# Layer 0: dt's products on four column groups of the array, and residual adds moved to TensorE and ScalarE

## The chip, the cores and the metric

The kernel runs on one core of one Trainium2 chip. The metric is the device time of one execution in microseconds (us), as the median of several runs. Engines are named as the profile names them: PE is TensorE's matmul, PEld its weight load, DVE is VectorE, ACT is ScalarE, POOL is GpSimd, SP is the queue that only issues DMAs. All data are float32.

## The reference, cut to what matters

The network has four layers of the form x = x + layer(groupnorm(x)) on an input of 1024 channels by 64 x 64. The change touches layer 0 alone, where the 1024 channels are also the sequence of a decaying sum:

```
def layer0(x, log_A, dt_w, dt_b, ln_w, ln_b):     # x after the group norm: [1, 1024, 64, 64]
    x_norm = layernorm2d(x, ln_w, ln_b)           # per channel, over the 64 x 64 image
    A = -exp(log_A)                               # one per image row
    dt = softplus(einsum('bsdc,c->bsd', x_norm, dt_w[0]) + dt_b[0])   # a sum over the 64 columns
    cums = cumsum(dt * A, axis=1)                 # along the channels
    M = exp(cums_t - cums_j) for t >= j, else 0   # per image row
    return einsum('btjr,bjrc->btrc', M, x_norm)
x = x + layer0(groupnorm(x))
```

dt is one number per channel and image row. The sum with M is a scan along the channels: out[t] = exp(dt[t] A) out[t-1] + x_norm[t]. Layers 1 to 3, mainly large matmuls, need mean and variance of layer 0's result first.

## The kernel before, in words

**Units and pieces.** Layer 0 works on 8 units u: four chunks of 256 channels (2 tiles k of 128 channels), each in two halves of the image (32 rows). A unit has 16 blocks of 128 pixels (32 rows by 4 columns), in 4 pieces g of 4 blocks. So there are 32 pieces, i = 4u + g, and the main loop (L753) runs once a piece.

**The steps of a piece.** A tile holds channels on its partitions. normalize (L581) writes xn, the group norm and layer norm in one scale and bias, on GpSimd for all but the first twelve. turn_in (L598) turns eight 128x128 blocks on TensorE into PSUM (tile xpt, two buffers), and ScalarE (in the first pieces partly VectorE) copies them to xt with ln_w and ln_b (four instructions of 128x256). Now pixels are on the partitions and channels along the row. row_dt (L617) makes dt: four products a piece, sixteen accumulated in PSUM tile pd of a unit; the weights dtm (128x128) hold dt_w and sum over the four columns of an image row and at once spread the sum to the four partitions of that row. decay (L625) is in three steps: step 0, four ScalarE instructions, makes softplus in two parts, e and m; step 1 adds them on TensorE, by two products with the identity, into the other half of pd; step 2 makes exp(A dt) (ScalarE, tiles first and a). begin (L646, GpSimd) puts the end of the chunk before into the first column. scan (L653, VectorE) runs two scans of 128x512. turn_back (L672) turns the eight blocks back into PSUM (tile pb, two buffers, one for each k), and add_up (L686) adds them to the image in place, with the sum of the result (VectorE; two instructions of 128x512). squares (L699, ScalarE) takes a finished tile's squares for the variance.

**by_act.** For k = 1 of pieces 25 to 30 the residual add goes otherwise (by_act, L665): TensorE first puts the image's piece into PSUM by a product with the identity (L676), then adds the four blocks by plain products instead of transposes (L682), and ScalarE copies the sum back with its total (L695).

**What sets the order.** The engines' orders are written out by hand (manual_schedule, L515): each engine runs its instructions in the order of the program. turn_in runs LEAD = 7 pieces ahead of scan, row_dt 6. In the loop's body the order is: normalize (for odd i, two tiles), decay step 1 (at g = 2), scan of i, add_up of i - 1, turn_in of i + 7, row_dt of i + 6, turn_back of i, decay step 0 of unit u + 1 (g = 1), decay step 2 and begin of unit u + 1 (g = 2), statistics of later units (VectorE, up to i = 11), one step of the next chunk's group norm (from i = 3 and 11), squares of unit u - 1 (g = 0 and 1), and one step of sums. sums (L711) prepares weights of layers 1 and 2 in the meantime: every four pieces four additions on GpSimd (L456 to L459), with their loads and stores on SP's queue. GpSimd's queue thus has, unit by unit: begin, the four additions, normalize.

Of the kernel before, what the change touches and what calls it, by code (L numbers as in the profile page):

```python
# [10 lines left out]
F32 = mybir.dt.float32  # L11
# [9 lines left out]
P = 128  # L21
# [16 lines left out]
NK = -(-N // LT)  # L38
# [27 lines left out]
T0 = HN // P  # L66
TR = HW // 2
TW = HW // T0
CH = 2
NPIECE = T0 // 4  # L70
# [4 lines left out]
        ("Alog", S), ("D", 1), ("mob", 4 * HEADS), ("dbcb", HEADS * NF)]  # L75

_CST = [("ident", P), ("fold", LC), ("same", P), ("upto", LC), ("far", LC), ("eye", LC), ("eye8", S),
        ("from", 1), ("to", NK), ("group", P), ("row", P),
        ("gx", NT), ("gy", NT), ("flip", 7)]


# [9 lines left out]
CST, NCST = _columns(_CST)  # L91
# [3 lines left out]
def tile_net(ctx: ExitStack, tc: tile.TileContext, x, par_d, cst_d, w_d, w2_d, dbcw_d, out):  # L95
    nc = tc.nc
# [23 lines left out]
    cst = const.tile([P, NCST], F32, name="cst")  # L120
    par = const.tile([P, NPAR], F32, name="par")
    ident = cst[:, CST["ident"]]
# [388 lines left out]
    with tc.issue_after(exp_ln.ins), tc.tile_pool(name="l0x", bufs=2) as lx, \  # L511
# [4 lines left out]
        NU, NI = CT // CH * 2, CT // CH * 2 * NPIECE  # L516
# [27 lines left out]
        negA0 = const.tile([P, 2], F32, name="negA0")  # L544
        nc.scalar.activation(negA0, par[:, PAR["logA"]], AF.Exp)
        negA = const.tile([P, S], F32, name="negA")
        nc.scalar.activation(negA, par[:, PAR["Alog"]], AF.Exp)
        dtm = l0.tile([P, T0, P], F32, name="dtm", bufs=1)
        for t in range(T0):
            nc.gpsimd.tensor_scalar(dtm[:, t, :], cst[:, CST["row"]], pcol("dtw", t), None, ALU.mult)  # L550
        carry = l0.tile([P, 2, T0], F32, name="carry", bufs=1)
# [24 lines left out]
            nc.vector.tensor_copy(mean0[:, at], mean)  # L576
            nc.vector.tensor_scalar_mul(nmean0[:, at], mean, -1.0)

        xn, XT, PD, dt, PB = {}, {}, {}, {}, {}

        def normalize(n):  # L581

# [34 lines left out]
        def row_dt(i):  # L617
            u, g = divmod(i, NPIECE)
            if g == 0:
                PD[u] = ps0.tile([P, FB], F32, tag="pd", name=f"pd{u}")  # L620
            for j in range(4):
                t = 4 * g + j
                nc.tensor.matmul(PD[u][:, : CH * P], dtm[:, t, :], XT[i][:, j, :], start=(t == 0), stop=(t == T0 - 1))  # L623

        def decay(u, step):  # L625

            if step == 0:
                e = l0.tile([P, CH * P], F32, tag="e", name=f"e{u}", bufs=1)
                m = l0.tile([P, CH * P], F32, tag="m", name=f"m{u}", bufs=1)
                dt[u] = e, m  # L630
                v = PD[u][:, : CH * P]
                nc.scalar.activation(e, v, AF.Abs, bias=pcol("dtb", 0))
                nc.scalar.activation(e, e, AF.Exp, scale=-1.0)
                nc.scalar.activation(m, v, AF.Relu, bias=pcol("dtb", 0))
                nc.scalar.activation(e, e, AF.Ln, bias=1.0)
            elif step == 1:
                for i, v in enumerate(dt[u]):
                    nc.tensor.matmul(PD[u][:, CH * P :], ident, v, start=(i == 0), stop=(i == 1))
            else:
                v, scale = PD[u][:, CH * P :], negA0[:, u % 2 : u % 2 + 1]  # L640
                if u > 1:
                    nc.scalar.activation(first_[u % 2], v[:, :1], AF.Exp, scale=scale)
                nc.scalar.activation(spread[u % 2][:, :, 1:], v[:, 1:].unsqueeze(1).to_broadcast([P, 2, CH * P - 1]),
                                     AF.Exp, scale=scale)
# [18 lines left out]
                nc.gpsimd.tensor_copy(carry[:, u % 2, 4 * g : 4 * g + 4], XT[i][:, :, CH * P - 1])  # L663

        def by_act(i, k):  # L665
            return NI - LEAD <= i < NI - 1 and k == 1

        def pieces_of(i, k):
            u, g = divmod(i, NPIECE)
# [42 lines left out]
        LEAD = 7  # L712
# [18 lines left out]
        row_dt(2)  # L731
        unit_stats(3, range(4))
        row_dt(3)
        decay(0, 0)
        normalize(4)
        unit_stats(3, range(4, 8))
# [16 lines left out]
        for i in range(NI):  # L753
            u, g = divmod(i, NPIECE)
            if i > 1 and i % 2 and i + LEAD + 2 < 4 * NU:
                normalize(i + LEAD + 2)
                normalize(i + LEAD + 3)
            if u + 1 < NU and g == 2:
                decay(u + 1, 1)
            scan(i)  # L760
            hand_on(i)
            if i == 0:
                finish_of(chain)
                chain = iter(())
            if i > 0:
                add_up(i - 1)
            if i == 0:
                for v, n in later.pop(0):
                    unit_stats(v, (n,))
                turn_in(5, (2, 3))  # L770
                turn_back(0)
                turn_in(6, (2, 3))
                row_dt(5)
            elif i + LEAD < NI:
                if i == 1:
                    row_dt(LEAD - 1)
                    turn_in(LEAD, (2, 3))
                    normalize(LEAD + 3)
                    normalize(LEAD + 4)
                turn_in(i + LEAD, ())  # L780
            if 0 < i <= NI - LEAD:
                row_dt(i + LEAD - 1)
            if i > 0:
                turn_back(i)
            if i == 0:
                normalize(LEAD + 1)
                normalize(LEAD + 2)
            if u + 1 < NU and g == 1:
                decay(u + 1, 0)
            if u + 1 < NU and g == 2:  # L790
                decay(u + 1, 2)
                if u > 0:
                    begin(u + 1)
            for v, n in later.get(i, ()):
                unit_stats(v, (n,))
            if i in (3, 11):
                chain = norm_chunk(2 if i == 3 else 3)
            next(chain, None)
            if i >= NPIECE and g < CH:
                squares(u - 1, g)  # L800
            if u == NU - 1 and 0 < g:
                for k in range(CH):
                    squares(u, k, g - 1)
            if g == 0 and u % 2 == 1:
                last_keep = keep(u // 2)
            if i == NPIECE + 1:
                bring(6)
            next(sums, None)
# [232 lines left out]
    with tc.manual_schedule(engines={E_.DVE, E_.PE, E_.Pool, E_.Activation}):  # L1041
        for i, _ in enumerate(pointwise("l1", W1, "b1", [3, 2] + EARLY, x0_d, x1_d, scores)):
# [11 lines left out]
            elif i == last - 1:  # L1054
                columns(FIRST, finish_of(chain), norm2)
                mv2 = moments("gn2b", SECOND, range(2))
                name = f"{WX}_{EARLY[0]}"
# [20 lines left out]
    part, silus = {}, []  # L1078
# [21 lines left out]
    with tc.tile_pool(name="l2a", bufs=2) as pa, tc.tile_pool(name="l2a2", bufs=1) as pa2, \  # L1100
# [5 lines left out]
        row = pa2.tile([P, TPB, HEADS, NF2], F32, name="row", bufs=1)  # L1106
# [729 lines left out]
def _constants():  # L1836
    c = np.zeros((P, NCST), np.float32)
    p, j = np.arange(P)[:, None], np.arange(P)[None, :]
    c[:, CST["ident"]] = p == j
    h, r = np.divmod(p, LC)  # L1840
    t = np.arange(LC)[None, :]
    c[:, CST["fold"]] = r == t
    c[:, CST["same"]] = h == j // LC
    c[:, CST["upto"]] = (t < S) | (r <= t)
    c[:, CST["far"]] = np.where((r >= S) & (t >= S) & (t < r), FAR, 0)
    c[:, CST["eye"]] = (r == t) & (r >= S)
    c[:KW, CST["eye8"]] = np.tile(np.eye(S), (KW // S, 1))
    c[:, CST["from"]] = HEADS * N + np.where(r < S, h * S + r, HEADS * S)
    c[:, CST["to"]] = HEADS * N + np.arange(NK)[None, :] * P + p
    c[:, CST["group"]] = (p // 32 == j // 32) / 32  # L1850
    c[:, CST["row"]] = p // TW == j // TW
    s = 1 - 2 * ((np.arange(P)[:, None] >> np.arange(6)[None, :]) & 1)
    s[:, 5] = 1
    c[:, CST["flip"]] = np.concatenate([s[:, :1], -s[:, :1], s[:, :5] * s[:, 1:]], axis=1)
    lin = _side()
    c[:, CST["gx"]] = np.tile(lin, HW).reshape(NT, P).T
    c[:, CST["gy"]] = np.repeat(lin, HW).reshape(NT, P).T
    return c
# [63 lines left out]
```

## Time and profile before

| | us |
|---|---|
| median of 3 runs | 2637.35 (2635.98 to 2638.56) |
| the profiled execution, its own time | 2640.7 |
| its span | 2638.5 |
| layer 0 ends, first matmul of layer 1 (L892) starts | 196.98 |
| first scan (L658) starts | 41.65 |
| one transpose block of turn_in, issue to issue | 0.12 |
| one scan (L658, 64 in all), mean | 1.205 |
| one residual add on VectorE (L697, 58 in all), mean | 0.68 |
| one residual add on ScalarE (L695, 6 in all), mean | 0.58 |
| products of dt (L623, 256 records), busy in all | 64.1 |

A row of the timeline or of the chain gives the start in us from the span's start, the length in us, the engine, the line and the tiles, with "x4" for four instructions in one row. In a row of the windows come, after the stretch and its length, each engine's busy time with its instructions in brackets, then the granted clock of TensorE (1.00 is full), the DMA engines' share and GB/s. A float32 product is two records of TensorE (two passes over the moving data each), a transpose is one. The durations of matmuls are modelled and overlap; the distance from start to start says what one costs.

### The profile page before, as it was taken

How to read it: one execution, taken by the hardware profiler on the slowest of the kernel's cores; microseconds unless marked ns; L12 is line 12 of the kernel's file. 1: busy time of each engine (PE TensorE's matmuls, PEld its weight loads, DVE VectorE, ACT ScalarE, POOL GpSimd, SP SyncE). 2: the span in 40 equal slices, each digit the busy share in tenths (PEclk: the TensorE clock that was granted, in tenths of full speed). 3: DMA queues.
4: the chain of work that ended last, by engine and by line, in shares of the span. 5: the costliest groups of instructions: out<-in, count | busy, mean ns of one | idle time of the engine just before them, and what ended most of it. 6: DMA issues, size and time to landing. Idle time of an engine off the chain costs nothing.

```text
span 2638.5 us, 30736 instructions
## 1 busy us (share of the span) xinstructions
PE 2560.3 (97%) x9588; PEld 1714.0 (65%) x9588; DVE 1819.1 (69%) x3776; ACT 1057.0 (40%) x1799; POOL 1217.9 (46%) x1102
## 2 busy tenths in 40 slices
PE   5889999999999999999999999999999999999999
PEld 5764444444555445544454558888888888788887
DVE  7986775664565554377877766576685775877877
ACT  4672010005655554476867662233233223312120
POOL 2453224322324242256464635576565665754544
PEclk9999999999999999999999999999999999999999
DMA  6555648655655676577677847899898798888896
GB/s 258 184 210 166 230 146 279 205 157 200 188 148 143 155 190 162 179 248 224 206 241 240 283 140 211 220 277 291 236 296 253 247 306 222 290 284 299 301 322 216
DMA packets 426996, 597.22 MB, mean 226 GB/s; under 512 B 142004, under 2 KB 210739, under 8 KB 423764
## 3 DMA queue, kind: packets, MB, share of 16 engines
q1 hardware_dynamic: 307268, 384.68, 46.0%
q10 hardware_dynamic: 91744, 136.85, 14.7%
q0 software_dynamic: 27824, 73.74, 11.7%
q8 instruction: 78, 1.28, 0.2%
q14 instruction: 82, 0.67, 0.1%
HBM read 435.10 MB, written 160.05 MB: 226 GB/s over the span
## 4 chain that ended last, share of the span: by engine, by line
PE 83%; DVE 8%; ACT 5%; POOL 1%; DMA 1%; issue 1%; SPq 0%; ACTq 0%; DVEq 0%; POOLq 0%
PE mm L892 38%; PE q_P2P L1793 6%; PE q_P3P L1793 5%; PE q_P1P L1793 5%; PE q_P5P L1793 5%; PE q_P6P L1793 5%; PE q_P4P L1793 5%; PE q_P7P L1793 5%; PE l2pt L1145 2%; PE py L1430 2%; DVE xt L658 1%; DVE cvp L1126 1%; ACT b L996 1%; DVE stats L567 1%; PE pd L623 1%
## 5 line engine op out<-in xcount | busy, mean ns | idle before, releaser
L892 PE MATMUL mm<-t,w 128*128 128x512 f32 x1536 | 681.0, 594 | 0.0
L892 PE MATMUL mm<-b,w 128*128 128x512 f32 x1152 | 513.6, 597 | 5.1 <-ACT b L996 4.0
L892 PEld LDWEIGHTS mm<-t,w 128*128 128x128 f32 x1536 | 285.8, 190 | 321.4 <-issue 313.6
L892 PEld LDWEIGHTS mm<-b,w 128*128 128x128 f32 x1152 | 215.6, 191 | 252.7 <-issue 240.7
L1439 POOL DMA_INDIRECT y_rows<-g,dst x74 | 74.1, 1001 | 181.8 <-ACT g L1435 169.9
L1126 DVE SCALAR_TENSOR_TENSOR cvp<-xs,par,cvp 128x512 f32<-128x512 f32 x128 | 95.4, 754 | 75.7 <-ACT cvp L1123 73.4
L1762 ACT COPY qQ<-q_P5P 128x512 f32<-128x512 f32 x48 | 28.1, 584 | 296.4 <-PE q_P5P L1793 269.0
L470 POOL TENSOR_TENSOR s<-s 128x256 f32<-128x256 f32 (+3 forms) x120 | 130.2, 1090 | 7.5
L1433 ACT COPY g<-py 8x512 f32<-8x512 f32 x146 | 83.8, 574 | 107.6 <-PE py L1430 106.6
L1177 DVE TENSOR_TENSOR xs<-mm,xs 128x512 f32<-128x512 f32 x64 | 41.8, 685 | 117.9 <-PE mm L892 117.9
L1153 POOL TENSOR_TENSOR acc<-l2xt,acc 128x136 f32<-128x136 f32 x56 | 29.3, 522 | 193.6 <-ACT l2xt L1147 192.7
L1013 DVE SCALAR_TENSOR_TENSOR image<-mm,par,image 128x512 f32<-128x512 f32 x64 | 47.0, 745 | 88.2 <-PE mm L892 88.2
L1145 PEld LDWEIGHTS l2pt<-both,cv 128*128 128x128 f32 x512 | 76.1, 190 | 34.6 <-issue 21.5
L850 POOL TENSOR_TENSOR t<-t,b 128x512 f32<-128x512 f32 x40 | 55.7, 1419 | 88.8 <-DVE t L850 85.4
L996 ACT ACTIVATE b<-image,gnl_bias,gnl_r_r 128x512 f32<-128x512 f32 x48 | 37.0, 808 | 145.4 <-PE mm L892 114.2
L1793 PE MATMUL q_P1P<-t_b,wq_P1P 128*128 128x256 f32 x384 | 92.0, 383 | 2.5 <-POOL t_b L1547 2.5
L1547 POOL TENSOR_TENSOR t_t<-qt 128x512 f32<-128x512 f32 x23 | 29.6, 1288 | 138.9 <-DVE qt L1547 72.4
L1793 PE MATMUL q_P5P<-t_t,wq_P5P 128*128 128x256 f32 x384 | 92.2, 383 | 0.4 <-POOL t_t L1547 0.4
L1793 PE MATMUL q_P4P<-t_t,wq_P4P 128*128 128x256 f32 x384 | 90.9, 380 | 1.4 <-DVE qV L1770 1.4
L1551 ACT ACTIVATE qb<-x_x_b,gn_bias,gn_r_r 128x512 f32<-128x512 f32 x64 | 48.8, 808 | 107.3 <-DVE qQ L1722 36.0
L1770 DVE TENSOR_TENSOR qV<-q_P4P,qV 128x512 f32<-128x512 f32 x96 | 64.8, 686 | 37.7 <-PE q_P4P L1793 36.0
L1793 PE MATMUL q_P6P<-t_t,wq_P6P 128*128 128x256 f32 x384 | 90.7, 379 | 0.0
(432 smaller groups left out, 5962.6 us busy)
## 6 DMA issues: line engine op xcount, KB each, us to landing
w<-s_d SPq DMA_DIRECT2D x96, 512.0 KB, 4.3
w<-in_w_dram SPq DMA_DIRECT2D x72, 512.0 KB, 4.7
x_x_b<-x_d ACTq DMA_DIRECT2D x28, 1024.0 KB, 6.4
image<-x_d SPq DMA_DIRECT2D x12, 2048.0 KB, 12.4
wq_P6P<-s_d SPq DMA_DIRECT2D x84, 256.0 KB, 4.3
wq_P7P<-s_d SPq DMA_DIRECT2D x84, 256.0 KB, 5.5
wq_P5P<-s_d SPq DMA_DIRECT2D x84, 256.0 KB, 3.1
wq_P3P<-s_d SPq DMA_DIRECT2D x84, 256.0 KB, 3.6
```

Source lines behind the costliest of these rows:

```text
L470: eng.tensor_tensor(out, a, b, ALU.subtract)
L850: eng.tensor_tensor(B[name][k], B[one][k], B[two][k], ALU.subtract)
L892: nc.tensor.matmul(to[o], w[:, k, o * P : (o + 1) * P], B[name][k], start=(fresh and k == 0), stop=(k == KH - 1), skip_group_check=True)
L996: nc.scalar.activation(t, X[nb][:, ct, :], AF.Identity, bias=bias, scale=scale)
L1126: nc.vector.scalar_tensor_tensor(cv, xo[:, at + t : at + t + FB], pcol("dww", 3 * o + t), cv, ALU.mult, ALU.add)
L1145: nc.tensor.matmul(pt[:, q * NV : (q + 1) * NV], cv[:, (q0 + q) * P : (q0 + q + 1) * P], both[:, o, :], start=True, stop=True)
L1430: nc.tensor.matmul(py, G2[k % 2], rows[k][:, :DH], start=True, stop=True)
L1433: nc.scalar.copy(rows[k + 1][h * LC : h * LC + S, :DH], py[h * LC : h * LC + S])
L1439: nc.gpsimd.indirect_dma_start(out=y_views[k % len(y_views)][:, :], out_offset=bass.IndirectOffsetOnAxis(ap=dst_[:, k : k + 1], axis=0), i ...
L1551: nc.scalar.activation(tile_of(j, name)[:, k], held[j, "x", name][:, k], AF.Identity, bias=bias, scale=scale)
L1770: nc.vector.tensor_tensor(to, ps, to, ALU.add)
L1793: nc.tensor.matmul(ps[:, o, :], w[:, k, o * P : (o + 1) * P], rhs[:, k, :], start=(new and o == 0 and k == 0), stop=(k == 1), skip_group_c ...
```

## The change

**dt's products.** dtm becomes 32 columns wide: its product gives one row of the result for each image row, without the spreading. The four products of a piece (j = 0 to 3) write four different groups of 32 partitions of pd, so each uses its own group of 32 columns of the array; every group accumulates over the four pieces of the unit. Two new steps make the whole of it: own_rows copies pd (128x256) to SBUF on ScalarE, and all_rows adds the four groups and spreads the rows with one product with a new constant, rows, into the other half of pd. decay reads that half, and its step 1 writes the first half.

**The order.** own_rows of unit u + 1 stands after row_dt and ahead of turn_back of the pieces with g = 1; all_rows after turn_back; then squares of unit u - 1, which at g = 1 were at the end of the body, and then decay step 0.

**The residual adds.** by_act now also holds for k = 1 of pieces 0 to 13. TensorE gets fourteen products with the identity and 56 plain products in place of transposes, ScalarE fourteen adds, VectorE loses fourteen.

```diff
-        ("from", 1), ("to", NK), ("group", P), ("row", P),
+        ("from", 1), ("to", NK), ("group", P), ("row", TR), ("rows", P),
...
-        dtm = l0.tile([P, T0, P], F32, name="dtm", bufs=1)
+        dtm = l0.tile([P, T0, TR], F32, name="dtm", bufs=1)
...
-                nc.tensor.matmul(PD[u][:, : CH * P], dtm[:, t, :], XT[i][:, j, :], start=(t == 0), stop=(t == T0 - 1))
+                nc.tensor.matmul(PD[u][j * TR : (j + 1) * TR, : CH * P], dtm[:, t, :], XT[i][:, j, :],
+                                 start=(g == 0), stop=(g == NPIECE - 1))
+
+        def own_rows(u):
+            part[u] = l0.tile([P, CH * P], F32, tag="m", name=f"part{u}", bufs=1)
+            nc.scalar.copy(part[u], PD[u][:, : CH * P])
+
+        def all_rows(u):
+            nc.tensor.matmul(PD[u][:, CH * P :], cst[:, CST["rows"]], part[u], start=True, stop=True)
...
-                v = PD[u][:, : CH * P]
+                v = PD[u][:, CH * P :]
...
-                    nc.tensor.matmul(PD[u][:, CH * P :], ident, v, start=(i == 0), stop=(i == 1))
+                    nc.tensor.matmul(PD[u][:, : CH * P], ident, v, start=(i == 0), stop=(i == 1))
...
-                v, scale = PD[u][:, CH * P :], negA0[:, u % 2 : u % 2 + 1]
+                v, scale = PD[u][:, : CH * P], negA0[:, u % 2 : u % 2 + 1]
...
         def by_act(i, k):
-            return NI - LEAD <= i < NI - 1 and k == 1
+            return k == 1 and (i < NI - 2 * LEAD - 4 or NI - LEAD <= i < NI - 1)
...
         row_dt(3)
+        own_rows(0)
+        all_rows(0)
         decay(0, 0)
...
                 row_dt(i + LEAD - 1)
+            if u + 1 < NU and g == 1:
+                own_rows(u + 1)
             if i > 0:
                 turn_back(i)
...
             if u + 1 < NU and g == 1:
+                all_rows(u + 1)
+                if i >= NPIECE:
+                    squares(u - 1, g)
                 decay(u + 1, 0)
...
-            if i >= NPIECE and g < CH:
+            if i >= NPIECE and g < CH and not (g == 1 and u + 1 < NU):
                 squares(u - 1, g)
...
-    c[:, CST["row"]] = p // TW == j // TW
+    c[:, CST["row"]] = p // TW == j[:, :TR]
+    c[:, CST["rows"]] = p % TR == j // TW
```

## The prediction

> **What bounds the kernel now.** I read the page's slices first, then a table by stretches, then the chain of waits inside layer 0 (0 to 197 us), where all of the change lies. From 197 us on TensorE hardly pauses:
>
> ```profile
> PE   5889999999999999999999999999999999999999
> DVE  7986775664565554377877766576685775877877
> ```
>
> A slice is 66 us: only the first three of PE are not full. What comes after layer 0 moves with its end, so one us won or lost there is one us of the run. Inside layer 0:
>
> ```profile
> core 0: us, PE busy (x) PEld busy (x) DVE busy (x) ACT busy (x) POOL busy (x), PEclk, DMA share, GB/s
> 41.60:75.20 33.60, 28.46 (x165) 24.87 (x165) 31.86 (x63) 23.27 (x41) 10.68 (x13) 0.95 0.13 49
> 75.20:93.60 18.40, 15.63 (x99) 13.81 (x98) 18.26 (x38) 13.16 (x29) 7.53 (x12) 1.00 0.84 302
> 93.60:113.90 20.30, 16.24 (x97) 14.04 (x96) 20.23 (x39) 13.80 (x27) 14.10 (x23) 0.92 0.35 121
> 113.90:131.80 17.90, 16.91 (x101) 15.04 (x100) 15.38 (x34) 12.29 (x25) 5.87 (x11) 0.90 0.49 174
> 131.80:149.40 17.60, 15.85 (x101) 14.07 (x101) 14.17 (x25) 13.76 (x27) 11.50 (x18) 1.00 0.38 127
> ```
>
> Until 113.9 us VectorE is full (31.86 of 33.60, 18.26 of 18.40, 20.23 of 20.30). Afterwards no engine is full, and yet a unit (four pieces) takes 17.3 us. The chain of waits of one such unit says why:
>
> ```profile
> 126.77 0.16 ACT first L642
> ...
> 127.09 0.32 POOL carry L648
> ...
> 128.15 1.22 POOL s_s L456
> ...
> 133.43 2.37 POOL xn L590 x2
> 135.80 0.04 issue
> 135.85 1.11 PE xpt L607 x7
> 136.96 1.74 PE pd L623 x8
> 138.70 0.02 issue
> 138.72 0.48 ACT e L632
> ...
> 140.31 1.71 ACT junk_None L709
> ...
> 142.30 1.82 ACT xt L615 x4
> 144.12 0.16 ACT first L642
> ```
>
> It is a **ring**: first lets GpSimd begin; that queue then runs the weight sums and the next xn; TensorE needs xn to turn in, then does pd; ScalarE does the decay, the squares, the four xt, and the next first. First starts at 85.68, 103.02, 126.66, 144.00, 161.33 and 175.33 us, so three of five turns are 17.34, 17.34 and 17.33: the ring binds from 85 to 103 us too, level with VectorE. The turn of 23.64 us is set by VectorE and the group norm's small products.
>
> **The change, part by part.**
>
> *VectorE.* One add (its read of the accumulator included) takes 0.60 us: two, as four rows, take 1.20 in the chain. Fourteen fewer: -8.4 us of VectorE, nearly all in stretches where it is full. It counts only where nothing else closes the gap.
>
> *TensorE, dt's products.* Now four products are eight records in 1.74 us a piece, 0.214 each. No product of the trace lies on 32 columns, so I bound it: 0.43 if all four groups run at once (two records after each other), 1.74 if none do. Both records of one product use the same columns, so if records also start in their order, the second of one overlaps only the first of the next: five steps of 0.214, **1.07 us**, the value I take, as it lies between the ends; both ends go into the range.
> The Trainium skill (TensorE: Matmul & The Clock Gate, Part 3) gives 2.38 times for three column tiles, and I estimate from it 0.55 us here; TensorEngine Tiling (Key Properties) speaks against: a switch of the tiling mode drains the array, twice a piece here, without a price.
>
> *TensorE, turning back.* The last pieces already add by TensorE:
>
> ```profile
> 171.08 1.02 PE L676 MATMUL pb<-low,cst 128*128 128x512 f32 x2
> 171.94 0.60 PE L684 MATMUL pb<-cst,xt 128*128 128x128 f32 x4
> 172.38 1.06 PE L682 MATMUL pb<-cst,xt 128*128 128x128 f32 x8
> 173.27 0.38 PE L638 MATMUL pd<-e,cst 128*128 128x256 f32 x1
> ```
>
> By the starts: 0.86 for the identity product, 0.44 for four transposes, 0.89 for four plain products. A piece costs 2.19 instead of 0.87, +1.32. With xpt 0.96, a changed piece takes 0.96 + 1.07 + 2.19 = 4.22 us of TensorE, where it was 3.57. The one residual add left on VectorE waits for the identity product first.
>
> *ScalarE.* Fourteen adds at 0.58 + 0.10 (174.76 to 175.43): they stand before the xt of the next piece and mostly fill waits for TensorE. The eight own_rows are copies of 128x256; the nearest rows are the Relu and Abs of the same shape from PSUM, 0.46 and 0.47. I take 0.47, with 0.58 (the 128x512 copy) as the other end.
>
> *The ring.* Four things happen to its turn.
> (a) pd gets 0.67 shorter, but own_rows stands behind the four xt in ScalarE's queue, and these end 2.53 us after xpt's start (135.85, 138.38), pd at 2.85. So own_rows starts at most 0.3 earlier: -0.3, whatever pd costs below 1.6.
> (b) own_rows: +0.47.
> (c) all_rows (one product, 0.43) comes after turn_back on TensorE and is hidden behind the squares (1.99 + 0.10), which now stand ahead of decay. Uncovered it would cost 0.43 and up to 2.19 of turn_back more.
> (d) The squares used to cover TensorE's answer to decay. TensorE does the sums of e and m (140.37 to 141.33, 0.96) and then xpt; xt starts 0.74 after xpt (144.89 to 145.63). Both now follow decay with nothing on ScalarE but an add: 0.06 + 0.96 + 0.74 = +1.76.
> Sum: -0.3 + 0.47 + 1.76 = **+1.9 us**, a turn of 19.3 instead of 17.34. New waits: ScalarE's for xt, with spread and first behind it, GpSimd behind those; TensorE's for e, 3 us instead of 0.8, with xpt behind it.
> In the changed pieces TensorE alone needs 4 x 4.22 + 0.43 + 0.96 + 2.1 (its wait for e: all_rows ends 4.65 after xpt's start, decay at 6.8) = 20.4 a unit, more than the ring.
>
> *The head.* Up to the first scan, shorter pd lets the statistics start about 1 us sooner; up to 85.68 VectorE loses five adds, -3.0. Against it stand 1.32 of turning back a piece, own_rows, all_rows and the uncovered waits of two decays. With pd at 1.07 the rows run so: turn_back of piece 3 ends at 69.6 (now 68.5); xpt of piece 11 runs to 72.0, in two halves with ScalarE's xt between, since a product of the group norm holds one of its two PSUM tiles (its gap now: 1.17); pd and turn_back take 1.07 + 2.19, to 75.2; xpt of piece 12, in halves again, to 77.7; pd 78.8; own_rows 79.3; squares 81.4; decay 83.0; sums of e and m 84.0; xt 84.7 to 86.5; first at **86.6**. With pd at 0.43 all of it is some 2.5 us earlier, 84. The 32-wide dtm saves GpSimd time before 21 us, where TensorE waits for ScalarE's xn, not for it: nothing. The 96 other columns of the constants: nothing, they land long before use.
>
> *The sum*, as times of first: 86.6 (+0.9); + 20.4 = 107.0 (+4.0); + 20.4 + 0.5 for the group norm's two products = 127.9 (+1.2: this turn was 23.64); + 19.3 = 147.2 (+3.2); + 19.3 = 166.5 (+5.2). Begin follows, and with it scan 24, 0.4 of whose delay an earlier wait had hidden (+4.8). From there VectorE paces the last eight pieces as now; its one wait of 0.72 at 176 goes. End of layer 0: **+4.1 us**, and as much on the run. With pd at 0.43 it starts 2.5 earlier, TensorE needs no more than the ring, and it ends at about 0.
> The profiled execution took 2640.7 (span 2638.5), 3.35 over the median of the runs, 2637.35. Nothing in the sum depends on that, so I add to the median: **2641.4 us**.
>
> **The rivals.** A measurement can tell 0.2%, 5.3 us, from no change.
>
> *The clock halves in the new waits (slower).* Two stretches show where this decides:
>
> ```profile
> 107.18:110.60 3.42, 1.46 (x11) 1.06 (x10) 3.42 (x7) 0.13 (x1) 3.34 (x3) 1.00 0.60 222
> 110.60:114.01 3.41, 2.47 (x8) 2.19 (x9) 3.34 (x9) 2.19 (x5) 3.25 (x6) 0.50 0.39 153
> 69.64:73.05 3.41, 2.08 (x13) 1.87 (x14) 3.41 (x8) 1.40 (x3) 0.55 (x2) 1.00 0.00 0
> ```
>
> 1.46 us busy of 3.42 (43%) was followed by half clock; 2.08 of 3.41 (61%), and 1.73 (51%) at 58 us, were not. With turning back at 0.87, all_rows ends at 3.55 after xpt's start and TensorE then waits till 6.8: 3.2 us idle. Half clock then doubles the e and m sums (+0.87) and half of xpt (+0.44): +1.3 a turn. It decides from a busy share somewhere between 43% and 51%. Two to five turns: 2644 to 2648, on to 2650 with more. Against it: where the windows fall is luck, and a window half in the wait keeps the clock.
> The skill's page on the clock gate (Part 1) has a free-running window of 3413 ns, which agrees with the 3.41 us of half clock here.
>
> *The groups don't overlap (slower; the change doesn't do what it says).* pd stays 1.74: a changed unit on TensorE is 4 x 4.89 + 0.43 + 0.96 + 1.65 = 22.6, +2.2 for two units, +1.5 in the head, +0.3 in the ring: 4.1 + 6.2 = +10.3, 2647.7. For it: no row shows overlap. Against it: the groups write different partitions.
>
> *The relief goes through (faster).* If the ring's waits are shorter than the order of the queues makes them, VectorE is what counts up to 114 us: -8.4, and some of its later 9.3 us of waits for pb goes as well. About -8, 2629. For it: VectorE is full there. Against it: GpSimd waits 25.0 us for first after 113 us alone, and the chain passes through it.
>
> **How the numbers follow.** The forecast (2641.4; 2637 with pd at 0.43) 0.42; half clock 0.25; no overlap 0.16; relief 0.17. The first is within 0.2%; I count both slower rivals as slower and the last as faster: 0.17, 0.42, 0.41. The range 2632 to 2651 leaves out the far half of the faster case and the mixtures of both slower ones, under 2 in 10.
>
> **What would show it.** pd on 32 columns: the spacing of a piece's eight records (0.43, 1.07 or 1.74). The turns of first: 19.3 instead of 17.34 after 126 us. ScalarE idle by about 1.7 us between decay's last step and the next xt. VectorE's adds 44 instead of 58, and waits for pb in pieces 6 to 12. Granted clock 0.5 between 125 and 170 us for the first rival. I am wrong if the turns stay near 17.3, or if first comes well before 84 us in its first turn.

## The result, and the profile after

The changed kernel takes **2643.83 us** (median of nine runs, 2642.00 to 2651.33) against 2637.35 before (median of nine, 2635.09 to 2638.90): a ratio of **1.0025, with a 95% interval of 1.0016 to 1.0034**, or 6.5 us longer. The forecast was 2641.4, 4.1 us longer; the range holds the time, and the loss lies a little beyond the 0.2% that the forecast's own case allowed.

The profiled execution took 2642.14 (span 2640.3), only 1.4 over the one before. That pair misleads. Layer 1's first product starts at 201.87 instead of 196.98, **+4.9 us**. The same instructions of the later layers are 4.2 us late up to 920 us (L351 on VectorE starts at 905.56 instead of 901.33) and 5.0 by 1570 us. The profile before then happens to have two more stretches of half clock in layer 3 (at 1574.9 and 2312.2 us, 3.4 us each), and after each of them the distance has shrunk by some 1.7 us. So layer 0 is where the change must be read, by the start of layer 1's first product; the rest of the span, from there on, takes 2438.0 to 2445.5 us in the fourteen profiles of this study, whatever was done to layer 0.

That start is itself good to a microsecond or two only. Ahead of it stands a row of small steps that make layer 1's group norm; from the first of them (tile mean, behind the last residual add) to the first product it is 6.0 to 8.6 us in the fourteen profiles. One of the steps in the profile before, beside an addition of the weight sums on GpSimd, and the same step in the changed kernel:

```profile
194.40 1.26 POOL L457 TENSOR_TENSOR s_a<-s_a,s_a 128x512 f32<-128x512 f32 x1
194.41 1.26 DVE L174 SCALAR_TENSOR_TENSOR gnl_r_t<-gnl_r_t,gnl_v 128x8 f32<-128x8 f32 x1
...
200.02 0.17 DVE L174 SCALAR_TENSOR_TENSOR gnl_r_t<-gnl_r_t,gnl_v 128x8 f32<-128x8 f32 x1
```

The step took 1.26 us there and 0.17 here. The residual adds themselves end later by more than 4.9: mean starts at 195.46 instead of 189.85, +5.6. Of this 1.1 came back by that step, and 0.4 was added by the first product's wait for its weights (a DMA, by the profile).

The page's slices of the changed kernel are like those shown of before, with small differences: VectorE's second and third are lower (8 7 where it was 9 8) and its fourth higher, as layer 0 ends later, and TensorE's third is lower (7, was 8):

```profile
PE   5879999999999999999999999999999999999999
...
DVE  7877775674565554377877766576585775877876
```

Three of the stretches that were shown of before, in the changed kernel (busy time of PE, PEld, DVE, ACT, POOL, then the clock):

```profile
75.20:93.60 18.40, 14.71 (x111) 10.41 (x109) 15.68 (x31) 13.50 (x33) 6.42 (x12) 1.00 0.65 233
93.60:113.90 20.30, 17.84 (x120) 12.84 (x116) 14.86 (x24) 15.46 (x33) 11.53 (x18) 0.92 0.33 107
...
131.80:149.40 17.60, 12.39 (x91) 8.72 (x91) 12.66 (x23) 13.12 (x26) 9.77 (x17) 0.90 0.35 120
```

VectorE is no longer full: 15.68 of 18.40 and 14.86 of 20.30, where it had 18.26 and 20.23. TensorE is less busy later on (12.39 of 17.60, where it had 15.85). And yet no unit is done sooner; from 131.8 to 149.4 us every engine is idle for a quarter of the time or more (ScalarE, the fullest, is busy for 13.12 of 17.60). The first of each unit starts at 86.79, 106.86, 128.25, 147.39, 167.30 and 180.55 us: turns of 20.07, 21.39, **19.14, 19.91** and 13.25. One such turn in the chain of waits of the changed kernel:

```profile
128.37 0.16 ACT first L650
...
135.03 2.36 POOL xn L590 x2
...
138.16 1.75 ACT xt L615 x4
...
139.97 0.38 ACT part L628
140.35 1.99 ACT junk_None L717 x2
...
143.52 0.31 ACT e L643
...
143.88 1.13 PE pd L646 x4
...
145.58 1.93 ACT xt L615 x4
```

Up to xt at 138.16 it is the ring of before: first, GpSimd up to xn, TensorE, ScalarE. New are own_rows (part, 0.38) and the steps on PE between e and xt (pd, the sums, and then 0.48 of xpt): the chain used to pass from decay through the squares to xt on ScalarE alone. It now goes over to TensorE and back, 143.83 to 145.58, while ScalarE stands still.

### The profile page after: what moved, and what is told of

The parts are those of the page before. It is cut to its first block, busy times and chain, and to the rows that moved or that the text cites. A ratio compares the mean times of both kernels' runs of the same rounds, so it can differ in the third digit from the quotient of the medians.

```text
span 2640.3 us, 30951 instructions
## 1 busy us (share of the span) xinstructions
PE 2551.5 (97%) x9688; PEld 1686.4 (64%) x9688; DVE 1804.8 (68%) x3748; ACT 1068.0 (40%) x1835; POOL 1214.2 (46%) x1102
## 4 chain that ended last, share of the span: by engine, by line
PE 84%; DVE 6%; ACT 6%; POOL 2%; DMA 2%; issue 1%; SPq 0%; ACTq 0%; DVEq 0%; POOLq 0%
PE mm L907 38%; PE q_P2P L1808 6%; PE q_P3P L1808 5%; PE q_P5P L1808 5%; PE q_P1P L1808 5%; PE q_P4P L1808 5%; PE q_P7P L1808 5%; PE q_P6P L1808 5%; PE py L1445 2%; PE l2pt L1160 2%; DVE cvp L1141 1%; ACT b L1011 1%; PE xpt L607 1%; PE pr L1406 1%; DVE stats L567 1%
## 5 line engine op out<-in xcount | busy, mean ns | idle before, releaser
L1808 PE MATMUL q_P7P<-t_t,wq_P7P 128*128 128x256 f32 x384 | 90.7, 379 | 0.0
L1808 PE MATMUL q_P2P<-t_b,wq_P2P 128*128 128x256 f32 x384 | 90.7, 379 | 0.0
```

Source lines behind the costliest of these rows:

```text
L1808: nc.tensor.matmul(ps[:, o, :], w[:, k, o * P : (o + 1) * P], rhs[:, k, :], start=(new and o == 0 and k == 0), stop=(k == 1), skip_group_c ...
```

## The experiments

Three theories. **Theory 1, the ring:** the turns of layer 0 are set by first, GpSimd, TensorE's turning in, ScalarE's decay and the next first; the change added a trip from ScalarE to TensorE and back that nothing covers (1.75 us), and own_rows. **Theory 2, the adds:** the fourteen residual adds load TensorE and ScalarE with more than they take from VectorE. **Theory 3, the clock:** TensorE's new waits fall on whole windows of the clock gate, and the half clock makes the loss.

All ratios are to the kernel before, run on the same chip (its median there was 2637.2 to 2639.5). The last three columns are from each run's profile; "behind mean" is the stretch from the start of mean to layer 1's first product, which varies by itself (above).

| run | edit | ratio, 95% | layer 1's first product, us | behind mean, us | third and fourth turn, us |
|---|---|---|---|---|---|
| before | | 1 | 196.98 | 7.13 | 17.34, 17.33 |
| after | the change | 1.0025 (1.0016 to 1.0034) | 201.87 | 6.41 | 19.14, 19.91 |
| 1 | the change without the adds | 1.0037 (1.0021 to 1.0052) | 204.10 | 7.94 | 20.20, 19.92 |
| 2 | before, with the adds | 1.0010 (1.0001 to 1.0018) | 199.26 | 6.98 | 17.35, 17.34 |
| 3 | the change, sums of e and m behind turn_in | 0.9993 (0.9984 to 1.0001) | 196.12 | 8.63 | 17.29, 17.30 |
| 4 | the change, weight sums later | 1.0001 (0.9992 to 1.0009) | 198.38 | 6.03 | 17.41, 18.15 |
| 5 | the change with 3 and 4 | 0.9973 (0.9964 to 0.9982) | 189.89 | 6.03 | 14.57, 15.57 |
| 6 | before, weight sums later | 0.9992 (0.9983 to 1.0001) | 193.46 | 6.04 | 15.86, 16.20 |
| 7 | 3 without the adds | 0.9994 (0.9985 to 1.0003) | 196.21 | 8.06 | 17.29, 17.29 |
| 8 | the change, squares behind decay | 1.0022 (1.0013 to 1.0031) | 203.52 | 6.88 | 19.23, 20.05 |
| 9 | the change, waits filled | 1.0059 (1.0046 to 1.0073) | 211.63 | 8.08 | 19.80, 19.79 |
| 10 | the change, once more | 1.0029 (1.0017 to 1.0041) | 205.91 | 8.64 | 20.76, 20.83 |
| 11 | before, with 3's edit | 1.0005 (0.9996 to 1.0014) | 197.43 | 7.51 | 18.72, 17.33 |
| 12 | before, with 2, 3 and 4 | 0.9994 (0.9985 to 1.0003) | 193.89 | 7.13 | 15.55, 15.24 |

### Runs 1 and 2: the two halves of the change

Run 1 keeps the column groups and drops the new adds; run 2 is the kernel before with the new by_act alone:

```diff
 run 1, from the changed kernel
-            return k == 1 and (i < NI - 2 * LEAD - 4 or NI - LEAD <= i < NI - 1)
+            return NI - LEAD <= i < NI - 1 and k == 1
 run 2, from the kernel before
-            return NI - LEAD <= i < NI - 1 and k == 1
+            return k == 1 and (i < NI - 2 * LEAD - 4 or NI - LEAD <= i < NI - 1)
```

> The changed kernel without its fourteen new adds on TensorE and ScalarE: dt on four column groups, own_rows, all_rows and the moved squares alone. Theory 1 (the ring from first through GpSimd's queue, xn, TensorE, ScalarE to the next first sets the time, and the moved squares and own_rows make its turn 1.9 us longer): the turns after 126 us stay at 19 to 20 us, the 85 to 126 us stretch goes back to being VectorE's, and the run is 4 to 8 us slower than before, 0 to +2 against the changed kernel. Theory 2 (TensorE, loaded with 1.3 us per piece by the new adds, makes the loss): the loss is gone, within 1.5 us of before or faster.

> The kernel before with only the fourteen new adds on TensorE and ScalarE; dt's products and the order of the decay as before. Theory 1: turns after 126 us are 17.3 us as before; up to there TensorE needs 4.9 us a changed piece (0.96 + 1.74 + 2.19), 21.4 a unit, so first at 126.66 comes 4 to 7 us later, and the run is 4 to 7 us slower than before. Theory 2: slower by as much as or more than the changed kernel (6.5 us), since without the column groups TensorE has less room. If the adds were free: faster than before by up to 8 us.

Without the adds the loss stays (1.0037, turns of 20.20 and 19.92): **theory 2 falls**. The groups with their order make it. The adds alone cost 2.3 us of layer 0, less than expected of them, and all of it ahead of the first turn (first at 87.96 instead of 85.68): the first changed turn grows from 17.34 to 19.98, with TensorE busy in all 19.98, but the next one shrinks from 23.64 to 21.12, because VectorE had set that one.

### Runs 3 and 11: the sums of e and m behind turn_in

```diff
-            if u + 1 < NU and g == 2:
-                decay(u + 1, 1)
             scan(i)
...
                 turn_in(i + LEAD, ())
+            if u + 1 < NU and g == 2:
+                decay(u + 1, 1)
             if 0 < i <= NI - LEAD:
                 row_dt(i + LEAD - 1)
```

Run 3 puts this into the changed kernel, run 11 into the kernel before. TensorE's xpt, and with it ScalarE's xt, then no longer stand behind the wait for e.

> The changed kernel with the sums of e and m (decay step 1) moved on TensorE behind turn_in of the same iteration, so that xpt is done while ScalarE still works on the decay and xt can follow at once. Theory 1: the 1.76 us between decay and xt go, turns after 126 us fall from 19.1 to 19.9 to 17.4 to 17.9 us, and the run is 5 to 8 us faster than the changed kernel, about level with before. Theory 2: TensorE's work is the same, so at most 2 us faster than the changed kernel. Theory 3 (half clock in the long waits makes the loss): the waits for e get shorter by xpt's 1 us, windows of half clock between 100 and 165 us go from three or four to none or one; the turn without half clock would stay at 19.1.

> The kernel before, with step 1 of decay (the sums of e and m) moved behind turn_in and row_dt in TensorE's order, as in the third run. Theory 1: here the squares stand between decay and xt on ScalarE and cover TensorE's answer already, so the moved sums win nothing: within 1.5 us of the kernel before, turns 17.0 to 17.4 us. If the move were a gain by itself (a better place of the sums, whatever stands on ScalarE), it would be 5 to 8 us faster than the kernel before, as the third run was against the changed kernel.

Run 3 wins the whole loss back. ScalarE's timeline of run 3 shows how (start, length, what; a wait would stand in brackets):

```profile
139.10 0.40 ACT L643 ACTIVATE e<-e 128x256 f32<-128x256 f32 x1
139.41 1.92 ACT L615 ACTIVATE xt<-xpt,par 128x256 f32<-128x256 f32 x4
```

xt follows e at once: TensorE turned in during the decay (xpt from 137.65 us), and the sums of e and m run while ScalarE copies xt. The two turns are 17.29 and 17.30 us, 1.85 and 2.61 below those of the changed kernel; 1.75 of it is the wait. There is half clock in these turns too, at 134.0 and 151.1 us, 3.4 us each; so the half clock alone does not bring the loss back. In the kernel before the same edit wins nothing (run 11), as theory 1 expects: there the squares already stand in the gap. Its turns are not all 17.0 to 17.4, though: the first and the third are 18.88 and 18.72. Each of them has a stretch of half clock inside (95.8 and 136.8 us), and the fourth, without one, takes 17.33.

### Runs 4, 5 and 6: the weight sums start a piece later

```diff
-            next(sums, None)
+            if i > 0:
+                next(sums, None)
```

This moves the four additions of a unit on GpSimd (5.3 us together, L456 to L459) by one piece, so that they stand behind the next xn instead of ahead of it. Run 4 does it to the changed kernel, run 6 to the kernel before, run 5 together with run 3's edit.

> The changed kernel with the weight sums started one iteration later, so that GpSimd runs the two xn ahead of the four additions (5.3 us) in each turn. Theory 1: the ring loses 5.3 us, turns after 126 us fall from 19 to 20 us to 14.5 to 16 us (VectorE needs 14.3), and the run is 6 to 10 us faster than the changed kernel, as fast as before or faster. Theory 2: GpSimd's order makes no difference, within 1.5 us of the changed kernel. Risk for both: the last sums come about 3 us later against the start of layer 1.

> The changed kernel with both orders altered: the sums of e and m behind turn_in, and GpSimd's weight sums one iteration later. Each alone brought the turns after 126 us to 17.3 and 17.4 to 18.2, the first limited by the ring, the second by ScalarE with its wait for xpt in it. Theory 1: with both, what is left is ScalarE's own work, 14.9 a turn, and VectorE's 14.3, so turns after 126 us take 15 to 16 us and the run is 3 to 6 us faster than with the sums behind turn_in alone, 2630 to 2633. If something third binds at 17.3, the run stays at 2636.

> The kernel before with GpSimd's weight sums one iteration later and nothing of the change. If the ring set its turns of 17.3 too, they fall to 15.5 to 16.5 after 126 us (TensorE has 15.2 of work in one, and 0.9 of waiting for e), and the run is 2 to 5 us faster than before. If VectorE or TensorE set them, the run stays within 1 us of before.

By layer 1's first product runs 4 and 6 gain 3.5 us each on what they start from, and run 5 gains 6.2 on run 3. Up to the start of mean the gains are 3.1, 2.4 and 3.6; the rest lies behind it, where in these three runs no addition of GpSimd falls beside the small steps (6.0 us in all three). In both kernels the turns get shorter, so GpSimd's part of the ring binds in both; run 6's ratio alone (0.9992, up to 1.0001) doesn't show a gain. In run 4 the turns fell by 1.7 only, not by the 3 to 4.6 expected: the uncovered trip is still there, and in that profile it is a wait of 2.82 for xpt, under half clock (141.8 us). **Run 5 beats both kernels**, 0.9973. Its first and third turns, as stretches:

```profile
85.31:103.69 18.38, 16.88 (x127) 12.39 (x126) 16.50 (x24) 16.20 (x36) 11.37 (x17) 1.00 0.56 188
...
123.36:137.93 14.57, 11.35 (x97) 8.20 (x95) 14.57 (x25) 13.91 (x28) 11.28 (x17) 1.00 0.41 140
```

In the third turn GpSimd has slack (11.28 of 14.57), VectorE is full (14.57 of 14.57), and ScalarE's only pauses in it are 0.20 and 0.43: the ring no longer sets the turn.

### Runs 7 and 12: what the parts are worth once the ring is short

Run 7 is run 3 with run 1's edit; run 12 is the kernel before with the edits of runs 2, 3 and 4, that is, run 5 without the column groups, own_rows, all_rows and the moved squares.

> The changed kernel with the sums of e and m behind turn_in and without the fourteen new adds on TensorE and ScalarE: what the adds are worth once the ring is short. Theory 1: after 126 us the turns stay at 17.3; before, VectorE has 8.4 us more, and the run is 1 to 5 us slower than with the adds (2635.9). If the adds do nothing for the time, it is within 1 us of that; if they cost, it is faster.

> The kernel before with everything of the fifth run but the column groups: the fourteen residual adds on TensorE and ScalarE, the sums of e and m behind turn_in, and the weight sums from i = 1 on. If the groups are worth something once the ring is short (theory 1 with TensorE as the next bound: in the run with the adds alone the first changed turn was 19.98 us with TensorE busy in all of it, and the groups take 1.17 us off each of its four pieces): turns of 19.5 to 21.5 us in the first two units where the fifth run had 18.4 and 19.7, layer 1's first product at 193 to 196 us, and a run 2.5 to 6 us slower than the fifth, a ratio to the kernel before of 0.998 to 0.9997. If all of the fifth run's gain is the two moves of the order and the adds: first two turns of 18.4 to 19.7, first product near 190 us, a ratio of 0.9965 to 0.998.

Run 7 cannot be told from run 3 (196.21 and 196.12 us, 0.9994 and 0.9993): with the ring at 17.3 the adds are worth nothing. Run 12 is 5.5 us slower than run 5 by the ratios (0.9994 to 0.9973) and 4.0 by layer 1's first product (2.9 by the start of mean). The first turn of run 12:

```profile
87.28:107.27 19.99, 19.99 (x124) 17.20 (x123) 15.78 (x23) 16.16 (x36) 11.33 (x17) 1.00 0.67 244
```

TensorE is busy from end to end, 19.99 of 19.99, and so it is in the second (21.12) and third turn (15.55). There the groups pay: they take 1.17 us from each of TensorE's four pieces of a unit, 9.4 in two units. With all_rows and the neighbours of pd, 6.0 of that is left in TensorE's busy time, and 3.1 shows in the first two turns (41.11 in run 12, 38.05 in run 5).

### Run 8: the squares put back behind the decay

```diff
                 all_rows(u + 1)
-                if i >= NPIECE:
-                    squares(u - 1, g)
                 decay(u + 1, 0)
...
-            if i >= NPIECE and g < CH and not (g == 1 and u + 1 < NU):
+            if i >= NPIECE and g < CH:
```

> The changed kernel with the squares of pieces with g = 1 back behind decay, as before the change, so that they again cover the sums of e and m and xpt. Then nothing covers all_rows: decay waits about 0.55 us for it in the late units and 1.4 us where turn_back holds the new adds. Theory 1: turns after 126 us of 18.0 to 18.3 instead of 19.1 to 19.9, the run 2 to 4 us faster than the changed kernel. If the moved squares were not the cause, it is as slow as the changed kernel or slower.

This one missed: 19.23 and 20.05, as slow as the changed kernel. Its ScalarE timeline shows why:

```profile
142.34 0.47 ACT L640 ACTIVATE e<-pd,par 128x256 f32<-128x256 f32 x1 [1.83 <-PE pd L631]
...
145.82 1.92 ACT L615 ACTIVATE xt<-xpt,par 128x256 f32<-128x256 f32 x4
```

xt follows the squares without a wait, as expected. But decay now waits 1.83 us for all_rows, which stands behind turn_back and, with it, under half clock (138.6 us on: turn_back took 1.76 from start to start where it takes 0.9). There are **two** trips to TensorE and back in the new order, own_rows to all_rows and decay to xt, and one pair of squares can cover only one of them. The prediction had priced the first, uncovered, at 0.43 and up to 2.19 of turn_back more; I expected 0.55 of it here and left out the half clock, to which some 0.9 of the 1.83 goes by turn_back alone. Both later turns of this profile have half clock in that place, so what they would take without it is not shown. In run 3's two turns there is no wait in either place.

### Run 9: TensorE's waits filled

```diff
+                if g == 1 and i > 13:
+                    idle = ps_tp(f"idle{i}")
+                    for _ in range(6):
+                        nc.tensor.matmul(idle[:, : CH * P], ident, XT[i - 1][:, 0, :], start=True, stop=True)
                 turn_in(i + LEAD, ())
...
                 all_rows(u + 1)
...
                 decay(u + 1, 0)
...
+                for _ in range(4):
+                    nc.tensor.matmul(PD[u + 1][:, : CH * P], ident, XT[i][:, 0, :], start=True, stop=True)
```

(The four products stand right behind all_rows.) Nothing reads the results of the added products.

> The changed kernel, with TensorE given products in its two waits of a unit whose results nothing reads: six identity products of 128x256 (0.43 us each) ahead of turn_in at g = 1 in units 4 to 6, and four after all_rows in every unit. They should keep the granted clock whole from 100 to 190 us, and they lengthen no wait (2.6 us in a wait of 2.66, 1.7 in one of 1.8 to 2.5). Theory 1 (the ring with the longer way from decay to xt): the two later turns stay at 18.5 to 19.4 us and the run is 0 to 2 us faster than the changed kernel. Theory 3 (the half clock in TensorE's new waits makes the loss): turns of 17.3 to 18 us and a run 4 to 6 us faster than the changed kernel.

The clock stayed whole from 83 to 206 us, as it was to. The third turn:

```profile
134.07:153.87 19.80, 16.97 (x124) 13.04 (x123) 14.12 (x25) 14.23 (x29) 11.27 (x17) 1.00 0.33 107
```

It is 19.80 at full clock, and the fourth 19.79. Of this 0.52 is the experiment's own: decay's first step waited that long for the four added products, which write its PSUM tile. That leaves 19.3, and the wait of the trip is the 1.75 us of the changed kernel:

```profile
152.05 1.93 ACT L615 ACTIVATE xt<-xpt,par 128x256 f32<-128x256 f32 x4 [1.75 <-PE xpt L607]
```

So **theory 3 falls** as the ground of the loss: at full clock, too, the ring makes a turn of 19.3. The run as a whole, 1.0059, tells nothing of the clock, against what I expected of it: in the head, where TensorE has no such wait to fill, the added products made first 4.9 us later.

### Run 10: the changed kernel once more

The kernel is the changed one as it is.

> The changed kernel as it is, beside the others on one chip. Both theories: 5 to 8 us slower than the kernel before (a ratio of 1.002 to 1.003), layer 0's later turns 19 to 20 us.

The ratio came again, 1.0029. This run's profiled execution was the longest of its six (2653.18 against a median of 2646.09). Of the 11.0 us that it took more than the first profile's, 7.1 lie behind layer 0. Its layer 0 is 4.0 us longer, 2.2 of them behind the start of mean; the turns are 20.71, 20.78, 20.76 and 20.83. A row of TensorE in its third turn, then ScalarE's next xt:

```profile
143.43 1.22 PE L646 MATMUL pd<-e,cst 128*128 128x256 f32 x2 [2.22 <-ACT e L643]
```
```profile
146.46 1.93 ACT L615 ACTIVATE xt<-xpt,par 128x256 f32<-128x256 f32 x4 [3.08 <-PE xpt L607]
```

Here the half clock (143.4 to 146.8 us) begins right as e arrives: the sums take 1.87 (to xpt at 145.30) instead of 0.97, and ScalarE waits 3.08 for xpt instead of 1.75, **+1.33 us**. That is the prediction's first rival, at its price of +1.3, on top of the ring and not in its stead. Which wait a window falls on differs from execution to execution of one and the same kernel: in the first profile it was the wait for xn (half clock at 138.1 and 155.2 us), which costs little, here also the one for e.

## Why the prediction was right, and where it was not

**What bounds, and the sum of the ring: right.** Step (d), "0.06 + 0.96 + 0.74 = +1.76", measured 1.75 in both later turns (the bracket on xt, at 145.58 and at 165.49):

```profile
145.58 1.93 ACT L615 ACTIVATE xt<-xpt,par 128x256 f32<-128x256 f32 x4 [1.75 <-PE xpt L607]
```

Step (a), -0.3, holds: from xpt to own_rows it is 2.54 (137.43 to 139.97), where from xpt to e it was 2.87 (135.85 to 138.72). Step (b), own_rows, was put at 0.47 and took 0.38. Step (c), all_rows hidden behind the squares, holds: decay's first step follows the squares at 142.22 without a wait; in the turn with half clock it waits 0.30. The turn was to be 19.3 and was 19.14 with one window of half clock, then 19.91 with two. Run 3, with run 11 beside it, shows that the uncovered trip is the cause, and run 9 that the clock is not needed for it; run 8 fits, but half clock blurs it.

**pd: mis-sized.** The step that failed is "the second of one overlaps only the first of the next: five steps of 0.214, 1.07 us". A changed piece on TensorE in the changed kernel, and a later one that has no pd:

```profile
89.22 0.64 PE L623 MATMUL pd<-xt,dtm 128*32 128x256 f32 x8
89.78 1.12 PE L684 MATMUL pb<-image,cst 128*128 128x512 f32 x2
90.75 0.60 PE L692 MATMUL pb<-cst,xt 128*128 128x128 f32 x4
...
180.35 1.02 PE L684 MATMUL pb<-low,cst 128*128 128x512 f32 x2
181.21 0.60 PE L692 MATMUL pb<-cst,xt 128*128 128x128 f32 x4
```

Read the distances from start to start: pd's eight records take 0.56 to 0.57 us, not 1.74. xpt ahead of them, from 88.16, takes 1.06 (it was 0.96), and the identity product behind them 0.97, where without pd it takes 0.86 (180.35 to 181.21). So a piece, from one xpt to the next (88.16 to 92.08), is 3.92 on TensorE, where I had 4.22 and the kernel before had 3.57. The rival "the groups don't overlap" falls. The Trainium skill (TensorE: Matmul & The Clock Gate, Part 3) would have given 0.55 by my estimate, and the trace agrees within 0.02; the price that TensorEngine Tiling (Key Properties) left open, a drain at each switch of the tiling mode, would be the 0.10 us on each side, if a switch is what these two distances show.

**The head: the better pd gave nothing back.** I had written that with pd at 0.43 "all of it is some 2.5 us earlier, 84", and that layer 0 then ends at about 0. pd was near that end, and first came at 86.79, not 84. The scan of piece 4 was indeed 1.6 us earlier than before (67.94 against 69.56). But in piece 12 of the changed kernel the second half of xpt has this row on TensorE:

```profile
77.47 0.75 PE L607 MATMUL xpt<-cst,xn 128*128 128x128 f32 x4 [2.01 <-DVE gn_v L213]
```

By the profile it waits 2.01 us until VectorE has read the group norm's product out of PSUM (gn_v, at 77.28). I had counted with the gap of before, 1.17, in that place: there the same half waits for ScalarE's xt alone and starts at 77.50, ahead of gn_v at 79.83. Why it waits for VectorE in the changed kernel is not shown. TensorE came to this piece earlier (74.75 instead of 75.63), and the longer wait took the gain back. Behind it comes the uncovered wait for e, 1.68 at 83.28. So the time of first was right (86.6 against 86.79) by two errors that cancel.

**The changed pieces.** The first turn was to be 4 x 4.22 + 0.43 + 0.96 + 2.1 = 20.4. It is 15.66 for the four pieces, 4.02 from there to the next xpt (99.91 to 103.93, with a wait of 2.46 for e in it, as pd's saving comes back as waiting), and 0.39 of half clock at 104.0: 20.07.

**VectorE: right in size, and worth nothing.** 44 adds instead of 58. The waits of 40 to 195 us before, then in the changed kernel (total, times, longest):

```profile
DVE image L697 <- PE pb L684: 5.2, 5, 1.9
DVE low L697 <- PE pb L684: 4.1, 3, 1.9
...
DVE low L705 <- PE pb L692: 12.3, 6, 4.6
...
DVE image L705 <- PE pb L692: 7.4, 6, 2.8
```

VectorE's waits for pb are 19.7 us in all, where they were 9.3: the 8.4 us of relief came back as 10.4 of waiting. GpSimd waits 44.9 us for first (31.1 before), TensorE 12.9 for e (5.8). The rival "the relief goes through" falls; run 1 has the same loss without any relief.

**The sum.** The firsts were to be 86.6, 107.0, 127.9, 147.2 and 166.5, and are 86.79, 106.86, 128.25, 147.39 and 167.30. The fourth turn, with its two windows of half clock, took 0.77 more than the third. The last term was wrong: "its one wait of 0.72 at 176 goes", but in the changed kernel that wait is 1.39 us (VectorE for pb, at 181.85), since in the last unit decay waits 0.97 for all_rows, which stands behind a turn_back with the adds. So mean starts 5.6 us later, where the end of layer 0 was put at +4.1. That layer 1's first product is at +4.9, and the layers behind it at +4.2, close to the forecast, is partly luck: the 1.1 us of the small step above, and a stretch of half clock at the start of layer 1 that covered less of its products than before (it lasted from 192.5 to 202.8 us before, with the first product at 196.98; now from 196.1 to 206.4, with the first product at 201.87).

The median's +6.5 may have more of the half clock in it: the nine runs reach up to 2651.33, and the mean clock was 0.990 and 0.991 in the two longest and 0.993 in the shortest. Only the first of the nine has a profile, so this is not shown; and in run 10's profile most of the extra time, 7.1 of 11.0 us, lay behind layer 0. The forecast treated the half clock as a rival, in which all or none of the executions would have it; the profile of run 10 and the first one show that it differs between executions of one kernel, and part of it belonged in the sum.

**The bound of the clock gate.** I had put it between 43% and 51% of TensorE's busy share in a window. A window of the changed kernel that was followed by half clock, and the next but one, which was not:

```profile
134.69:138.10 3.41, 1.05 (x6) 0.86 (x7) 3.41 (x7) 0.77 (x2) 3.41 (x6) 1.00 0.80 280
...
141.51:144.92 3.41, 1.64 (x8) 1.15 (x8) 3.04 (x6) 2.28 (x6) 0.00 (x0) 1.00 0.06 22
```

1.05 of 3.41 (31%) led to half clock, as 0.98 (29%) did from 151.74 us; 1.64 (48%), with the wait for e inside, did not. In run 10 the same wait fell otherwise into its window, 1.21 of 3.42 (35%), and half clock followed. Two windows of run 11 show that this share alone doesn't decide:

```profile
92.41:95.82 3.41, 2.00 (x12) 1.09 (x10) 3.41 (x7) 2.29 (x3) 3.41 (x5) 1.00 0.82 273
116.30:119.71 3.41, 1.54 (x9) 1.44 (x10) 3.38 (x9) 1.30 (x4) 1.02 (x2) 1.00 1.03 313
```

The first, 2.00 of 3.41 (59%), was followed by half clock; the second, 1.54 (45%), was not. So there is no sharp bound in TensorE's busy share as the profile gives it, and the prediction's 43% to 51% was too narrow a place to look: of the windows at full clock between 41 and 185 us in the fourteen profiles, all under 45% were followed by half clock and none above 59% was, and between them both happen. What else counts was not tried.

**Still open:** why the wait in the head changed from ScalarE to VectorE; why half clock followed the windows in the first and third turn of run 11 and whether it alone makes them 1.4 to 1.5 us longer; and how much of the head's 2.01 us wait for the group norm goes back to the longer half clock at its start (39.1 to 45.9 us instead of 42.3 to 45.7). None of this was tried.

## What to carry to other kernels

Look for trips from one engine to another and back in the chain that binds, and count them before and after a change: work that stands in such a gap covers it at no cost, and a change that moves this work to a second gap opens the first. When an engine that is full is relieved, find out first what its neighbours wait for; here 8.4 us came back as waits, until two moves of a line each (the sums of e and m behind turn_in, the weight sums a piece later) shortened the ring, and only then did the column groups pay. Compare profiles at the end of the changed stage, not by their spans, where stretches of half clock elsewhere can hide a few us; and take more than one instruction there, since the last small steps of a stage can differ by a microsecond or two with what runs beside them.

## What the runs showed of the hardware that was not expected

Four products of 128x256 on four groups of 32 columns, two records each, ran in 0.57 us from start to start, 3.05 times as fast as the same products on 128 columns (1.74), and the neighbours on full columns started 0.10 us later on each side. In ten of the fourteen profiles, one to three of the small steps of VectorE (128x8) ahead of layer 1 took 0.47 to 1.27 us instead of 0.16 to 0.17; each of these eighteen ended within 0.03 us of the end of an addition of 128x512 on GpSimd.

Executions of one kernel on one chip differed by up to 14.2 us (2644.11 to 2658.28 in run 1; 9.5 in run 10, 2643.70 to 2653.18), and in the profile of run 10's longest every one of layer 0's four long turns was 20.7 to 20.8 us instead of 19.1 to 21.4.
